# Layer 1 of a two-layer scan-convolution network: result units of one image group with all blocks of h, in place of units of two groups with half of the blocks

## The chip, the cores and the metric

The kernel runs on one core of one Trainium2 chip. The metric is the device time of one execution in microseconds. Three runs of the kernel before took 4558.59 to 4567.19 us, with a median of 4567.16. The profiled execution, from which all other times here come, spans 4551.0 us at a mean granted TensorE clock of 0.964.

## The reference

The input `x` has 32 images, 48 channels, 64 rows (h) and 128 columns (w), in float32. Two layers with weights of their own do the same thing:

```
x = x + SCNN(groupnorm16(x))

SCNN:  down   scan over h, from row 0 to 63
       up     scan over h, from row 63 to 0
       right  scan over w, from column 0 to 127
       left   scan over w, from column 127 to 0

one step of every scan:  nxt = inp + conv1d(carry, w, b)
```

In the down and up scans the convolution runs along w, in the right and left scans along h. It has 48 channels in and out, five taps and zero padding of two. Each step needs the step before it, so a layer is a chain of 63 + 63 + 127 + 127 steps for every image. The last operation of a layer adds its input `x`, the residual, to what the left scan leaves. After layer 1 that sum is the output.

## The kernel before

**Tiles.** The 32 images form four groups of eight (`GB`). One group fills the 512 columns of a matmul together with the eight blocks that a row or a column is cut into. The 384 partitions needed, 8 positions e inside a block times 48 channels, are three sets of 128 (o = 0, 1, 2). Since 48 doesn't divide 128, `pieces(o)` lists the 3 or 4 runs of partitions with one e each: 48, 48 and 32 channels, or 16, 48, 48 and 16.

**Steps.** A step is nine fp32 products on TensorE (L661) and three additions of bias and input on VectorE (L670). The products of the next step read what these additions wrote.

**Phases.** `PHASES` lists twelve, one after the other on TensorE. A "rows" phase does the down and up scans of one group (steps named d and u), a "cols" phase the right and left scans of a pair of groups (r and l). The last three are phase 9 (rows of group 3 in layer 1), phase 10 (columns of groups 0 and 1) and phase 11 (columns of groups 2 and 3). In the profile `step_13u` is the end of phase 9, `step_10r` and `step_10l` are phase 10, and `step_11r` and `step_11l` are phase 11.

**The arena.** One large SBUF tile holds three slots of 6 MB and four staging tiles of 1 MB (`stage`). A slot holds a quarter of w (32 columns) of a pair of groups, that is six units of 128 partitions by 2048 values (`UNITS` numbers them by o and by the half, which is the group in the pair). A column phase has four quarters and three slots: quarter 3 takes the slot of quarter 0. So quarter 0 is written to DRAM after the right scan has passed it (`spill_unit`, `spill<-arena`) and brought back during the left scan (`arena<-spill`). Two column phases in a row use the slots in opposite order, so that the quarters of phase 11 move into slots as phase 10 finishes with them. Their data come from DRAM, where the rows phases left them (`arena<-upb`; the stores are `upb<-arena`).

**Results of layer 1.** The left scan finishes quarters 3, 2, 1 and 0 in this order. Every unit of a quarter then goes through three functions:

- `load_residual` brings the unit's part of the layer's input from DRAM (`mid`) into a "nat" tile. There are three of these: two staging tiles, and the tile `downs`, which holds the weights of the rows scans until phase 9 is over. In layer 1 these loads are on ScalarE's DMA queue (`arena<-mid`, `downs<-mid`).
- `add_permuted` has GpSimd add the residual and put the values in the order of the output, w innermost, into one of two "perm" tiles: eight instructions of 128 by 256 (L621).
- `store_result` writes the perm tile to `out` (`out<-arena`), in runs of 32 values = 128 bytes, half of the transfers on SyncE's queue and half on ScalarE's. For quarters 2, 1 and 0 of phase 10 (`HELD`) it is `hold_result` instead, which writes long runs to a DRAM tile (`held<-arena`, SyncE). `let_result` copies these from DRAM to `out` during phase 11 (`out<-held`).

In layer 1 a unit is (o, r): both groups of the pair, and half (r) of the eight blocks of h. The final quarter of phase 11 is done after the last step by `last_loads` and `last_results` (L892 to L912), which use VectorE for the addition and ScalarE, GpSimd and VectorE for the copies that permute.

**Order.** All this work is entered in an agenda, `at(t, ...)`, with a due time counted in steps: the first three residual loads of a column phase at `left + 16`, where `left` is the first step of the left scan; the addition of unit i of the n-th finished quarter at `left + 34 + 32 n + 4.5 i`; its store or hold five steps later; the let-go copies of phase 10 from `end + 63` on. The agenda is sorted, the steps of the scans are put between, and `in_order` (L193) ties every instruction to the one before it on its engine. So each engine's own order is fixed. How the engines' instructions stand to each other is left to a scheduler. Two things follow from this:

- An engine's queue issues its transfers in order. A transfer that has to wait holds up all that stand behind it on that queue.
- The program has eight completion counters for the transfers of SyncE's and ScalarE's queues together. They are given out in turn in the scheduler's order. A transfer is issued only when the one before it on the same counter has landed, whichever queue that one is on.

Nearly all transfers go through the helper `dma` (L189), so the profile shows them with its line and tells them apart by the names of the tiles. In the changed program the helper stands at L192.

Of the kernel before, what the change touches and what calls it, by code (L numbers as in the profile page):

```python
# [29 lines left out]
F32 = mybir.dt.float32  # L30
AF = mybir.ActivationFunctionType
ALU = mybir.AluOpType

C = 48
# [7 lines left out]
GB = 8  # L42
E8 = 8
FULL = 128
NG = E8 * C // FULL
NQ = 4
# [45 lines left out]
def kernel(  # L92
# [56 lines left out]
    def kept(name):  # L149
# [14 lines left out]
        for i in range(4)  # L164
    ]

    HELD = (2, 1, 0)
    held = {
        j: dram.tile([C, 2 * CHANNEL // NQ], F32, tag=f"held{j}", name=f"held{j}") for j in HELD
    }  # L170

    def by_row(t, e, h0, h1):
# [10 lines left out]
    def by_col(t, e, j):  # L183


        return t.rearrange("c (i q n) -> i q c n", i=E8, q=NQ)[e, j]

    def dma(dst, src, queue=None):
        (queue or nc.sync).dma_start(dst, src)  # L189
# [21 lines left out]
    def pieces(o):  # L211
        return [(e, c0, c1, p0) for e, c0, c1, g, p0 in PIECES if g == o]
# [335 lines left out]
    def quarter(k, j):  # L548
        return slot[slots(k)[j % 3]].rearrange("p (o s n) -> p s o n", s=2, o=NG)
# [22 lines left out]
        else:  # L572
            dma(there, here)

    HH = NH // 2

    def load_residual(k, j, i, nat):
        _, layer, pair = PHASES[k]  # L580
        if layer == 0:
            o, half = UNITS[i]
            t = source[0][2 * pair + half]
            for e, c0, c1, p0 in pieces(o):
                dma(nat[p0 : p0 + c1 - c0], by_col(t, e, j)[c0:c1])
            return
        o, r = divmod(i, 2)
        view = nat.rearrange("p (s n) -> p s n", s=2)
        part = slice(r * HH * LINE, (r + 1) * HH * LINE)
        for e, c0, c1, p0 in pieces(o):  # L590
            for s in range(2):
                dma(
                    view[p0 : p0 + c1 - c0, s],
                    by_col(source[1][2 * pair + s], e, j)[c0:c1, part],
                    nc.scalar,
                )

    def add_residual(k, j, i, nat):
        o, half = UNITS[i]
# [9 lines left out]
                quarter(k, j)[p0 : p0 + c1 - c0, half, o],  # L609
            )  # L610

    def add_permuted(k, j, i, nat, perm, engines):
        o, r = divmod(i, 2)
        res = quarter(k, j)[:, :, o].rearrange(
            "p s (a e k b) -> p a s b k e", a=NH, e=E8, b=GB
        )[:, r * HH : (r + 1) * HH]
        inp = nat.rearrange("p (s a e k b) -> p a s b k e", s=2, a=HH, e=E8, b=GB)
        dst = perm.rearrange("p (a s b k e) -> p a s b k e", a=HH, s=2, b=GB, e=E8)
        for a in range(HH):
            for s in range(2):  # L620
                engines[(2 * a + s) % len(engines)].tensor_tensor(  # L621
                    dst[:, a, s], res[:, a, s], inp[:, a, s], ALU.add
                )

    def store_result(k, j, i, perm):
        pair = PHASES[k][2]
        o, r = divmod(i, 2)
        both = out[2 * pair * GB : 2 * (pair + 1) * GB]
        dst = both.rearrange("b c (a e) w -> e a c b w", e=E8)[..., j * WQ : (j + 1) * WQ]
        src = perm.rearrange("p (a b n) -> p a b n", a=HH, b=2 * GB)  # L630
        for a in range(HH):
            for e, c0, c1, p0 in pieces(o):
                to = nc.sync if a < HH // 2 else nc.scalar
                dma(dst[e, r * HH + a, c0:c1], src[p0 : p0 + c1 - c0, a], to)

    def hold_result(j, i, perm):
        o, r = divmod(i, 2)
        n = 2 * GB * WQ
        dst = held[j].rearrange("c (a e n) -> e c a n", e=E8, n=n)[:, :, r * HH : (r + 1) * HH]
        for e, c0, c1, p0 in pieces(o):  # L640
            dma(dst[e, c0:c1], perm[p0 : p0 + c1 - c0].rearrange("p (a n) -> p a n", n=n))

    def let_result(j, b, part):

        src = held[j][part].rearrange("c (h b n) -> b (c h) n", b=2 * GB, n=WQ)
        dst = out[b, part].rearrange("c h w -> (c h) w")
        dma(dst[:, j * WQ : (j + 1) * WQ], src[b])


    def step(key, weights, b_at, src, inp, dst, whole, part):  # L650
# [89 lines left out]
    def at(t, fn, *args):  # L740
        agenda.append((t, len(agenda), fn, args))
# [68 lines left out]
    def plan_cols(k, t0, prev):  # L810
# [39 lines left out]
        for u, (t, j, i) in enumerate(units):  # L850
            nat = nats[u % ahead]
            o, half = UNITS[i]
            if u < ahead:
                at(left + 16, load_residual, k, j, i, nat)
            elif not (final and j == 0):
                at(units[u - ahead][0] + (3 if layer == 0 else 4.9), load_residual, k, j, i, nat)
            if layer == 0:
                at(t, add_residual, k, j, i, nat)
                at(t + 4, keep_result, k, j, i)
                unit = quarter(k, j)[:, half, o]  # L860
                if half == 0:
                    for b in range(GB):
                        at(t + 5 + b, stats[0].take, j, o, unit, b)
                else:
                    at(t + 1, stats[1].take, j, o, unit)
            elif not (final and j == 0):
                perm = perms[u % 2]
                at(t, add_permuted, k, j, i, nat, perm, [nc.gpsimd])
                if final or j not in held:
                    at(t + 5, store_result, k, j, i, perm)  # L870
                else:
                    at(t + 5, hold_result, j, i, perm)
        if layer == 0:
            t = units[-1][0] + 14
            g = 2 * pair
            spread(t, scaling(f"r{g}", 1, g, stats[0], r_masks), 1)
            spread(t + 20, scaling(f"r{g + 1}", 1, g + 1, stats[1], r_masks), 1)
        if layer and not final:
            for n in range(len(HELD) * 4 * GB):
                n_done, i = divmod(n, 4 * GB)  # L880
                part = slice(i % 2 * C // 2, (i % 2 + 1) * C // 2)
                at(end + 63 + 0.95 * n, let_result, HELD[n_done], i // 2, part)
        if final:
            at(left + 97, last_loads, k)
            at(end + 4, last_results, k)
# [10 lines left out]
    def last_results(k):  # L896

        for i, nat in enumerate(last_tiles(k)):
            o, r = divmod(i, 2)
            part = slice(r * HH * LINE, (r + 1) * HH * LINE)  # L900
            unit = quarter(k, 0)[:, :, o, part]
            nat = nat.rearrange("p (s n) -> p s n", s=2)
            nc.vector.tensor_tensor(unit, unit, nat, ALU.add)
            src = unit.rearrange("p s (a e k b) -> p a s b k e", a=HH, e=E8, b=GB)
            perm = stage[:, i % 4]
            dst = perm.rearrange("p (a s b k e) -> p a s b k e", a=HH, s=2, b=GB, e=E8)
            for a in range(HH):
                for s in range(2):
                    eng = (nc.scalar, nc.gpsimd, nc.vector)[(2 * a + s) % 8 % 3]
                    copy = eng.copy if eng is nc.scalar else eng.tensor_copy  # L910
                    copy(dst[:, a, s], src[:, a, s])  # L911
            store_result(k, 0, i, perm)  # L912


# [227 lines left out]
```

## Time and profile before

| stretch | from, us | to, us | length, us |
|---|---|---|---|
| right scan, phase 10 | 3294.1 | 3593.5 | 299.4 |
| left scan, phase 10 | 3593.5 | 3849.0 | 255.4 |
| right scan, phase 11 | 3848.8 | 4170.6 | 321.8 |
| left scan, phase 11 | 4170.6 | 4426 | 255.4 |
| from the last step to the end | 4426 | 4551.0 | 125 |

A line of the first part of the page gives an engine's busy time, its share of the span and its number of instructions. The second part cuts the span into 40 slices of 114 us; a digit is the busy share in tenths. A line of a timeline gives the start, the length, the engine, the line, the operation with its output and input, the number of instructions in the stretch, and in brackets the idle time ahead of it with what ended it. A line of waits gives what waited, what it waited for, the total in us, the number of waits and the longest. `SPq` and `ACTq` are the queues on which SyncE and ScalarE issue transfers; `PEld` is TensorE's loading of weights.

GpSimd's additions for phase 11 begin at 4232.6 us. From then until the end of the span it adds 18 units, and the last six are added and copied by `last_results`. From 4422.15 to 4461.4 us ScalarE's queue issues the 48 residual loads of `last_loads`.

Transfers by kind, with the size of one and the median time from issue to landing:

| transfer | queue | count | KB each | us to landing |
|---|---|---|---|---|
| residual loads of layer 1 (arena<-mid) | ScalarE | 136 | 192 | 4.5 |
| stores (out<-arena) | SyncE | 120 | 96 | 3.4 |
| stores (out<-arena) | ScalarE | 120 | 96 | 3.2 |
| holds (held<-arena) | SyncE | 36 | 384 | 5.1 |
| let-go copies (out<-held) | SyncE | 96 | 192 | 4.4 |
| quarters (arena<-upb) | SyncE | 96 | 384 | 10.6 |
| spill (spill<-arena) | SyncE | 24 | 1024 | 13.1 |

The table lists the commonest size of each; a piece of 32 or 16 partitions makes smaller ones.

### The profile page before, as it was taken

The numbers are of one execution on the slowest core, as the hardware profiler recorded it, in microseconds if no ns is written. First come the engines' busy times: TensorE is split into PE (matmuls) and PEld (weight loads), VectorE is DVE, ScalarE is ACT, GpSimd is POOL, SyncE is SP. The second block draws the span as 40 slices with busy tenths as digits, with TensorE's granted clock in tenths as the row PEclk, the third lists the DMA queues.
The fourth block names the chain that finished last, engine by engine and source line by source line (L and its number), as shares of the span: only waits on it lengthen the run. The fifth ranks groups of instructions, "written<-read, shape, count | busy, mean of one in ns | idle before, by whom it ended". The sixth has DMA issues, their size and how long they took to land.

```text
span 4551.0 us, 90606 instructions
## 1 busy us (share of the span) xinstructions
PE 4164.5 (92%) x36632; PEld 4133.9 (91%) x36632; DVE 2182.1 (48%) x6594; ACT 1190.0 (26%) x2358; POOL 906.5 (20%) x943
## 2 busy tenths in 40 slices
PE   4899998999999999979999999999969998879990
PEld 1899998999999999979999999999969998879980
DVE  5354443446654444434456654444434444334441
ACT  1743302426776444000035944230000000000000
POOL 4351001314422020000024200000000055500453
PEclk9899998999999999989999999999989999989995
DMA  9989789858979999488048989393097079898789
GB/s 175 177 164 157 115 152 197 198 95 250 213 158 160 160 156 156 75 162 187 1 125 237 200 129 156 45 147 59 9 168 176 1 173 215 188 240 130 158 154 161
DMA packets 2133091, 680.41 MB, mean 150 GB/s; under 512 B 2009792, under 2 KB 2062784, under 8 KB 2101184
## 3 DMA queue, kind: packets, MB, share of 16 engines
q1 hardware_dynamic: 1984832, 602.23, 68.8%
q10 hardware_dynamic: 147840, 72.39, 7.8%
q8 instruction: 288, 4.72, 0.5%
q14 instruction: 131, 1.07, 0.1%
HBM read 397.57 MB, written 295.98 MB: 152 GB/s over the span
## 4 chain that ended last, share of the span: by engine, by line
PE 83%; DMA 9%; POOL 2%; SPq 2%; ACT 1%; issue 1%; ACTq 1%; DVE 1%; POOLq 0%; DVEq 0%
PE step_00r L661 6%; PE step_01r L661 6%; PE step_00l L661 6%; PE step_01l L661 6%; PE step_10r L661 6%; PE step_11l L661 6%; PE step_11r L661 4%; PE step_10l L661 3%; PE step_02u L661 3%; PE step_11d L661 3%; PE step_11u L661 3%; PE step_10u L661 3%; PE step_13u L661 3%; PE step_13d L661 3%; PE step_12u L661 3%; PE step_12d L661 3%
## 5 line engine op out<-in xcount | busy, mean ns | idle before, releaser
L532 ACT ACTIVATE arena<-arena,offset,scale 128x256 f32<-128x256 f32 (+2 forms) x864 | 601.4, 792 | 428.9 <-DMA arena<-mid 174.5
L489 POOL COPY arena<-arena 112x256 f32<-112x256 f32 x458 | 270.7, 647 | 755.4 <-DMA arena<-in_x 459.8
L911 ACT COPY arena<-arena 128x256 f32<-128x256 f32 x18 | 10.4, 643 | 1483.9 <-DMA out<-arena 1475.5
L621 POOL TENSOR_TENSOR arena<-arena 128x256 f32<-128x256 f32 x224 | 232.7, 1082 | 830.7 <-DVE arena L670 733.0
L601 POOL TENSOR_TENSOR arena<-arena 128x2048 f32<-128x2048 f32 x48 | 217.7, 4560 | 833.4 <-PE step_01l L661 537.5
L661 PE MATMUL step_11r<-arena,wright 128*128 128x128 f32 x2286 | 265.0, 280 | 56.9 <-DVE arena L670 30.6
L661 PEld LDWEIGHTS step_11r<-arena,wright 128*128 128x128 f32 x2286 | 263.5, 197 | 58.3 <-DVE arena L670 43.0
L423 ACT ACTIVATE junk<-arena 128x256 f32<-128x256 f32 x192 | 129.5, 675 | 692.6 <-DMA arena<-xin 552.3
L661 PE MATMUL step_10r<-arena,wright 128*128 128x128 f32 x2286 | 261.1, 278 | 38.5 <-DVE arena L670 27.0
L661 PEld LDWEIGHTS step_10r<-arena,wright 128*128 128x128 f32 x2286 | 260.2, 195 | 39.3 <-DVE arena L670 27.5
L661 PE MATMUL step_00r<-arena,wright 128*128 128x128 f32 x2286 | 257.9, 276 | 26.7 <-DMA arena<-upa 26.7
L661 PEld LDWEIGHTS step_00r<-arena,wright 128*128 128x128 f32 x2286 | 257.6, 193 | 27.0 <-issue 26.9
L661 PE MATMUL step_01r<-arena,wright 128*128 128x128 f32 x2286 | 257.3, 276 | 24.5 <-DMA arena<-upa 24.5
L661 PEld LDWEIGHTS step_01r<-arena,wright 128*128 128x128 f32 x2286 | 257.0, 193 | 24.8 <-issue 24.7
L661 PE MATMUL step_00l<-arena,wleft 128*128 128x128 f32 x2286 | 256.3, 275 | 0.0
L661 PEld LDWEIGHTS step_00l<-arena,wleft 128*128 128x128 f32 x2286 | 255.7, 192 | 0.0
L661 PE MATMUL step_11l<-arena,wleft 128*128 128x128 f32 x2286 | 255.4, 275 | 0.0
L661 PE MATMUL step_01l<-arena,wleft 128*128 128x128 f32 x2286 | 255.4, 275 | 0.0
L661 PE MATMUL step_10l<-arena,wleft 128*128 128x128 f32 x2286 | 255.4, 275 | 0.0
L661 PEld LDWEIGHTS step_11l<-arena,wleft 128*128 128x128 f32 x2286 | 255.4, 192 | 0.0
L661 PEld LDWEIGHTS step_01l<-arena,wleft 128*128 128x128 f32 x2286 | 255.3, 192 | 0.0
L661 PEld LDWEIGHTS step_10l<-arena,wleft 128*128 128x128 f32 x2286 | 255.3, 192 | 0.0
(174 smaller groups left out, 7106.1 us busy)
## 6 DMA issues: line engine op xcount, KB each, us to landing
xin<-arena SPq DMA_DIRECT2D x96, 384.0 KB, 5.5
arena<-xin SPq DMA_DIRECT2D x96, 384.0 KB, 8.4
mid<-arena SPq DMA_DIRECT2D x96, 384.0 KB, 7.8
arena<-mid SPq DMA_DIRECT2D x192, 192.0 KB, 4.3
upb<-arena SPq DMA_DIRECT2D x192, 192.0 KB, 4.0
arena<-upb SPq DMA_DIRECT2D x96, 384.0 KB, 10.6
arena<-xin SPq DMA_DIRECT2D x186, 192.0 KB, 4.4
upa<-arena SPq DMA_DIRECT2D x180, 192.0 KB, 3.9
```

Of the source, the lines that this page charges most:

```text
L423: nc.scalar.activation(junk[:, 0:n], view[:, b], AF.Identity, accum_out=self.sum[:, i, j : j + 1])
L489: copy(dst[:, r, q], src[:, r0 + r, q])
L532: nc.scalar.activation(args[0], args[0], AF.Identity, bias=args[2], scale=args[1])
L601: nc.gpsimd.tensor_tensor(unit, unit, nat, ALU.add)
L621: engines[(2 * a + s) % len(engines)].tensor_tensor(dst[:, a, s], res[:, a, s], inp[:, a, s], ALU.add)
L661: nc.tensor.matmul(part(whole(ps[o]), -s), weights[:, i, FULL * (o - NG * s - i + 1) : FULL * (o - NG * s - i + 2)], part(src(i), s), star ...
L911: copy(dst[:, a, s], src[:, a, s])
```

## The change

A unit of layer 1 becomes (o, half), as in layer 0: one group, all eight blocks of h. It is still 128 partitions by 2048 values, and GpSimd's additions are still eight of 128 by 256 to a unit. The purpose is to have fewer and larger transfers:

- A residual load is 3 or 4 transfers with runs of 8 KB, in place of 6 or 8 with runs of 4 KB. It stays on ScalarE's queue.
- A store is 3 or 4 transfers, all on SyncE's queue, in place of 12 or 16 on two queues. Each needs the whole unit, where a transfer before needed two of the eight additions. The runs in `out` stay at 128 bytes.
- A hold is one transfer of 1 MB on ScalarE's queue, in place of 3 or 4 on SyncE's, since `held` is now laid out by units. A let-go copy takes one e of one group: 48 copies in place of 96, with the same bytes in all.
- In layer 1 ScalarE gets a one-element copy, due at `left + 10`, that reads the last column of quarter 3's first block (column 120), which the left scan writes in its seventh step. Since ScalarE's instructions are in order, its residual loads come after that step.
- `last_results` follows the same units. Its copies go to the three engines in turn, a store of a unit stands behind them.

```diff
--- before.py
+++ after.py
@@ -164,9 +164,12 @@
         for i in range(4)
     ]
 
+
     HELD = (2, 1, 0)
     held = {
-        j: dram.tile([C, 2 * CHANNEL // NQ], F32, tag=f"held{j}", name=f"held{j}") for j in HELD
+        (j, half): dram.tile([NG, FULL, UNIT], F32, tag=f"held{j}{half}", name=f"held{j}{half}")
+        for j in HELD
+        for half in range(2)
     }
 
     def by_row(t, e, h0, h1):
@@ -572,28 +575,12 @@
         else:
             dma(there, here)
 
-
-
-    HH = NH // 2
-
     def load_residual(k, j, i, nat):
         _, layer, pair = PHASES[k]
-        if layer == 0:
-            o, half = UNITS[i]
-            t = source[0][2 * pair + half]
-            for e, c0, c1, p0 in pieces(o):
-                dma(nat[p0 : p0 + c1 - c0], by_col(t, e, j)[c0:c1])
-            return
-        o, r = divmod(i, 2)
-        view = nat.rearrange("p (s n) -> p s n", s=2)
-        part = slice(r * HH * LINE, (r + 1) * HH * LINE)
+        o, half = UNITS[i]
+        t = source[layer][2 * pair + half]
         for e, c0, c1, p0 in pieces(o):
-            for s in range(2):
-                dma(
-                    view[p0 : p0 + c1 - c0, s],
-                    by_col(source[1][2 * pair + s], e, j)[c0:c1, part],
-                    nc.scalar,
-                )
+            dma(nat[p0 : p0 + c1 - c0], by_col(t, e, j)[c0:c1], nc.scalar if layer else None)
 
     def add_residual(k, j, i, nat):
         o, half = UNITS[i]
@@ -609,42 +596,41 @@
                 quarter(k, j)[p0 : p0 + c1 - c0, half, o],
             )
 
-    def add_permuted(k, j, i, nat, perm, engines):
-        o, r = divmod(i, 2)
-        res = quarter(k, j)[:, :, o].rearrange(
-            "p s (a e k b) -> p a s b k e", a=NH, e=E8, b=GB
-        )[:, r * HH : (r + 1) * HH]
-        inp = nat.rearrange("p (s a e k b) -> p a s b k e", s=2, a=HH, e=E8, b=GB)
-        dst = perm.rearrange("p (a s b k e) -> p a s b k e", a=HH, s=2, b=GB, e=E8)
-        for a in range(HH):
-            for s in range(2):
-                engines[(2 * a + s) % len(engines)].tensor_tensor(
-                    dst[:, a, s], res[:, a, s], inp[:, a, s], ALU.add
-                )
+    def by_image(t):
+
+        return t.rearrange("p (a e k b) -> p a b k e", a=NH, e=E8, b=GB)
+
+    def by_w(t):
+        return t.rearrange("p (a b k e) -> p a b k e", a=NH, b=GB, e=E8)
+
+    def add_permuted(k, j, i, nat, perm):
+        o, half = UNITS[i]
+        res = by_image(quarter(k, j)[:, half, o])
+        for a in range(NH):
+            nc.gpsimd.tensor_tensor(by_w(perm)[:, a], res[:, a], by_image(nat)[:, a], ALU.add)
+
+    def in_output(j, g, e):
+
+
+        t = out[g * GB : (g + 1) * GB].rearrange("b c (a e) w -> e (c a) b w", e=E8)
+        return t[e, :, :, j * WQ : (j + 1) * WQ]
 
     def store_result(k, j, i, perm):
         pair = PHASES[k][2]
-        o, r = divmod(i, 2)
-        both = out[2 * pair * GB : 2 * (pair + 1) * GB]
-        dst = both.rearrange("b c (a e) w -> e a c b w", e=E8)[..., j * WQ : (j + 1) * WQ]
-        src = perm.rearrange("p (a b n) -> p a b n", a=HH, b=2 * GB)
-        for a in range(HH):
-            for e, c0, c1, p0 in pieces(o):
-                to = nc.sync if a < HH // 2 else nc.scalar
-                dma(dst[e, r * HH + a, c0:c1], src[p0 : p0 + c1 - c0, a], to)
+        o, half = UNITS[i]
+        for e, c0, c1, p0 in pieces(o):
+            dst = in_output(j, 2 * pair + half, e)[c0 * NH : c1 * NH]
+            src = perm[p0 : p0 + c1 - c0].rearrange("p (a b n) -> p a b n", a=NH, b=GB)
+            dma(dst.rearrange("(c a) b n -> c a b n", a=NH), src)
 
     def hold_result(j, i, perm):
-        o, r = divmod(i, 2)
-        n = 2 * GB * WQ
-        dst = held[j].rearrange("c (a e n) -> e c a n", e=E8, n=n)[:, :, r * HH : (r + 1) * HH]
-        for e, c0, c1, p0 in pieces(o):
-            dma(dst[e, c0:c1], perm[p0 : p0 + c1 - c0].rearrange("p (a n) -> p a n", n=n))
-
-    def let_result(j, b, part):
-
-        src = held[j][part].rearrange("c (h b n) -> b (c h) n", b=2 * GB, n=WQ)
-        dst = out[b, part].rearrange("c h w -> (c h) w")
-        dma(dst[:, j * WQ : (j + 1) * WQ], src[b])
+        o, half = UNITS[i]
+        dma(held[j, half][o], perm, nc.scalar)
+
+    def let_result(j, half, e):
+
+        src = held[j, half].rearrange("o p (a b n) -> (o p a) b n", a=NH, b=GB)
+        dma(in_output(j, half, e), src[e * C * NH : (e + 1) * C * NH])
 
 
     def step(key, weights, b_at, src, inp, dst, whole, part):
@@ -865,8 +851,8 @@
                     at(t + 1, stats[1].take, j, o, unit)
             elif not (final and j == 0):
                 perm = perms[u % 2]
-                at(t, add_permuted, k, j, i, nat, perm, [nc.gpsimd])
-                if final or j not in held:
+                at(t, add_permuted, k, j, i, nat, perm)
+                if final or j not in HELD:
                     at(t + 5, store_result, k, j, i, perm)
                 else:
                     at(t + 5, hold_result, j, i, perm)
@@ -875,11 +861,13 @@
             g = 2 * pair
             spread(t, scaling(f"r{g}", 1, g, stats[0], r_masks), 1)
             spread(t + 20, scaling(f"r{g + 1}", 1, g + 1, stats[1], r_masks), 1)
+        if layer:
+
+            at(left + 10, nc.scalar.copy, junk[:, 0:1], quarter(k, 3)[:, 0, 0, RUN - 1 : RUN])
         if layer and not final:
-            for n in range(len(HELD) * 4 * GB):
-                n_done, i = divmod(n, 4 * GB)
-                part = slice(i % 2 * C // 2, (i % 2 + 1) * C // 2)
-                at(end + 63 + 0.95 * n, let_result, HELD[n_done], i // 2, part)
+            todo = [(j, half, e) for j in HELD for half in range(2) for e in range(E8)]
+            for n, what in enumerate(todo):
+                at(end + 63 + 1.9 * n, let_result, *what)
         if final:
             at(left + 97, last_loads, k)
             at(end + 4, last_results, k)
@@ -896,19 +884,14 @@
     def last_results(k):
 
         for i, nat in enumerate(last_tiles(k)):
-            o, r = divmod(i, 2)
-            part = slice(r * HH * LINE, (r + 1) * HH * LINE)
-            unit = quarter(k, 0)[:, :, o, part]
-            nat = nat.rearrange("p (s n) -> p s n", s=2)
+            o, half = UNITS[i]
+            unit = quarter(k, 0)[:, half, o]
             nc.vector.tensor_tensor(unit, unit, nat, ALU.add)
-            src = unit.rearrange("p s (a e k b) -> p a s b k e", a=HH, e=E8, b=GB)
             perm = stage[:, i % 4]
-            dst = perm.rearrange("p (a s b k e) -> p a s b k e", a=HH, s=2, b=GB, e=E8)
-            for a in range(HH):
-                for s in range(2):
-                    eng = (nc.scalar, nc.gpsimd, nc.vector)[(2 * a + s) % 8 % 3]
-                    copy = eng.copy if eng is nc.scalar else eng.tensor_copy
-                    copy(dst[:, a, s], src[:, a, s])
+            for a in range(NH):
+                eng = (nc.scalar, nc.gpsimd, nc.vector)[a % 3]
+                copy = eng.copy if eng is nc.scalar else eng.tensor_copy
+                copy(by_w(perm)[:, a], by_image(unit)[:, a])
             store_result(k, 0, i, perm)
```

## The prediction

> **What bounds the kernel now.** The shares by engine and the slices come first.
>
> ```profile
> PE 4164.5 (92%) x36632; PEld 4133.9 (91%) x36632; DVE 2182.1 (48%) x6594; ACT 1190.0 (26%) x2358; POOL 906.5 (20%) x943
> PE   4899998999999999979999999999969998879990
> DMA  9989789858979999488048989393097079898789
> ```
>
> TensorE is busy 92% of the span, and the edit leaves its 36632 records alone. What can be won is its idle time: the digits 6, 8, 8, 7 in slices 29 to 37, where layer 1's column phases run, and the last 1.1 slices (125 us), where it is done and results still leave. The first 3040 us run the same instructions in the same order in both programs. Next, TensorE's stretches from 3280 us on.
>
> ```profile
> 3306.68 65.44 PE L661 MATMUL step_10r<-arena,wright 128*128 128x112 f32 x570 [11.48 <-DMA arena<-upb]
> 3381.15 1.65 PE L661 MATMUL step_10r<-arena,wright 128*128 128x128 f32 x6 [9.04 <-DVE arena L670]
> 3400.78 192.92 PE L661 MATMUL step_10r<-arena,wright 128*128 128x112 f32 x1702 [17.98 <-DVE arena L670]
> 3593.53 255.43 PE L661 MATMUL step_10l<-arena,wleft 128*128 128x128 f32 x2286
> 3864.93 66.15 PE L661 MATMUL step_11r<-arena,wright 128*128 128x112 f32 x570 [15.07 <-DMA arena<-upb]
> ...
> 4170.55 255.44 PE L661 MATMUL step_11l<-arena,wleft 128*128 128x128 f32 x2286
> ```
>
> A scan without waits takes 255.4 us (both left scans). Right scan 10 runs 3294.1 to 3593.5 = 299.4 us, 44.0 too long: 38.5 idle, the rest matmuls slowed after the pauses. Right scan 11 runs 3848.8 to 4170.55 = 321.75, 66.3 too long. The tail is 4551 - 4426 = 125. These three, 235 us, are all that the edit can touch. Who held the loads? SyncE's queue waits from 3060 to 3320 us, its timeline there, and GpSimd's waits from 3590 to 4060 and from 4170 on:
>
> ```profile
> SPq L189 <- DMA downs<-mid: 195.4, 4, 193.9
> ```
>
> ```profile
> 3078.51 220.98 SPq L189 DMA_DIRECT2D arena<-upb  x20
> 3299.86 55.19 SPq L189 DMA_DIRECT2D upb<-arena  x50
> ```
>
> ```profile
> POOL arena L621 <- DMA held<-arena: 88.9, 4, 40.8
> ```
>
> ```profile
> POOL arena L621 <- DMA out<-arena: 123.2, 18, 38.3
> ```
>
> SyncE stood 193.9 us behind a residual load (downs<-mid) that is not even on its queue, while DMA moved 1 GB/s (3160 to 3280 us, share 0.00). As soon as phase 9 ended it threw out 50 stores that had piled up, ahead of the next quarters. The built program says why: eight completion counters go in turn to the transfers of both queues, and a transfer waits for the one before it on its counter. The scheduler put ScalarE's residual loads of phase 10 far ahead; the one into `downs` waits for the last matmul of phase 9, which reads weights there, and SyncE's load of arena<-upb is next on that load's counter.
>
> **The Trainium skill.** "DMA: Bandwidth & Descriptors", section "Anatomy of one DMA — SWDGE (gpsimd) path", says that DMA engines never wait on semaphores; the issuing sequencer does, and what is queued behind it stands. The trace agrees: 193.9 us of queue, DMA share 0.00. Section "Issuing engines are not separate DMA queues": transfers of all issuers run on the same 16 engines, and a second issuer saves issue time alone. The trace agrees: stores on SyncE alone moved 159 GB/s (3320 to 3360), on both queues 154 (4470 to 4551). Section "Rules for kernel authors" advises to coalesce, with mostly overhead below 64 KB; here 96-KB stores land in 3.2 to 3.4 us and 384-KB holds in 5.1. Section "Specifications" asks for 512 B or more for line rate; the change keeps the 128-B runs of `out`, so I give its stores no better rate: 150 to 160 against 301 GB/s for loads with 8-KB runs (3440 to 3480).
>
> **The change part by part.**
>
> 1. *ScalarE's copy at left + 10.* It reads the seventh step of the left scan, so ScalarE's residual loads come after it, and the far hoisting ends. In the list of the changed program SyncE's two loads behind the stall wait for counters last held by SyncE's own loads. New wait: queued behind it are the residual loads alone, and GpSimd needs the first at left + 62 us (4232.6 - 4170.55), against about 14 us for seven steps: hidden by 45 us. The copy itself is one element: nothing. Gain: stores of phase 9 and loads of quarters 0 to 2 move into the 120 us in which DMA idled. Layer 0's right scans show one pause each, 26.7 and 24.5 us at the start, since their second group has only just been stored; phase 10's groups have long been stored, so even that is absent. I take all 44 (bounds 38, the idle alone, and 44).
>
> 2. *Holds: 3 or 4 of 256 to 384 KB on SyncE become one of 1 MB on ScalarE.* GpSimd adds a unit in 8 x 1.04 = 8.3 us into one of two perm buffers. Its 24 units took 335 us (3655 to 3990), 14.0 each, because holds lay in SyncE's order between loads of phase 11 that wait for quarters these very adds free. Now only residual loads share their queue. A 1-MB hold lands in 13.1 us (price of the 1-MB spill); bounds 5.1 and 22 (its queue full). Pace (8.3 + 13.1)/2 = 10.7 us; three residual buffers, (8.3 + 10.6)/3 = 6.3, don't bind. With S = start of the left scan: quarter 2 is summed at S + 62 + 12 x 10.7 = S + 190, its successor loaded (6 MB at 301 GB/s, 21 us) by S + 215, needed at S + 255. Quarter 1: S + 255, loaded S + 280, needed S + 319. Quarter 0: S + 319; then spill (6 MB) and load (6 MB), which the order puts behind step 31 of right scan 11, 42 us at full rate and some 60 beside holds: S + 361 to 379, needed S + 383. Close: I leave 8 of the 66 standing and take 58 (bounds 31 and 66).
>
> 3. *let_result: 48 of 384 KB for 96 of 192.* The same bytes in 128-B runs: 18.9 MB in 130 us (4060.5 to 4191). They start when quarter 3 is loaded, run into the left scan as now, and end before the first stores at left + 62. Nothing.
>
> 4. *Stores and residual loads of phase 11, and last_results.* A store was 12 to 16 transfers over both queues and could start on half a unit; now 3 or 4 on SyncE, for the whole unit. Lost is the overlap of add and store inside a unit; won, that GpSimd waits for fewer counters and that 48 last loads (39.2 us of ScalarE's queue at 4422) stand ahead of no store: GpSimd idled 38.3 us for that. But DMA is nearly full here: 4240 to 4340 at 0.91, to 4420 at 0.82, 4430 to 4468 and 4470 to 4551 at 1.03 make, with 4420 to 4430 counted full, 91 + 66 + 10 + 39 + 83 = 289 us of work in 311. Packed without holes that saves 22; 8-KB instead of 4-KB runs in 24 MB of loads some 8 more, my estimate. I take 30. Bounds: 0 (whole-unit stores leave as many holes), and 60, if stores at 160 and loads at 301 GB/s cost no more than 6.5 and 3.5 us a unit: 24 x 10.0 + 21 for the spill brought back = 261 from left + 62, so left + 323, against left + 380 now.
>
> 5. *Issue counts* (ScalarE some 340 transfers fewer, SyncE 208) and the DVE add and copies of last_results, same bytes: off the path, beside stores.
>
> Sum: 44 + 58 + 30 = 132; 4567 - 132 = **4435 us**.
>
> **Rivals.**
> - *B, only the stall of phase 9 goes:* DMA is full in 10 left and 11 right, holds land in 20 us, the pace stays near 14, and quarters 1 and 2 are still late. For: share 0.8 to 1.0 in the tail; 60 us of spill and load in a 64-us gap. Against: the longest waits before were for order. 44 + 20 + 10 = 74: 4493.
> - *C, slower:* whole-unit stores wait their turn in one queue with the spill coming back, each 22 us: (8.3 + 22)/2 = 15.2 a unit over 24 units = 364 against 318 now, +46; the same in phase 10 makes 11 right 20 worse; less 44: 4589. For: half-unit starts and the second queue are gone. Against: one queue alone kept 159 GB/s.
> - *D, everything fits:* 44 + 66 + 60 = 170: 4397. Against: 289 us of DMA work in the tail.
>
> **How the numbers follow.** Forecast 0.62, B 0.20, D 0.12, C 0.06. The range runs from D to B, 4393 to 4497, and leaves out C and the edges of the others. Faster by over 0.2%: A, B, D less a little for an order I misread, 0.92; within 0.2%: 0.02; slower: 0.06.
>
> **What would show it.** Step 1: no SyncE wait of over 20 us before 3300, right scan 10 at 255 to 261 us. Step 2: GpSimd's waits for held under 40 us in all, units 10 to 11.5 us apart, right scan 11 at 255 to 275, any pause at quarter 2. Step 4: GpSimd's 18 units of phase 11 at 11 to 12.5 us, tail 85 to 105. I would be wrong if ScalarE's queue, where holds now wait for GpSimd ahead of residual loads, starved GpSimd of residuals, or if a counter shared across queues stalled SyncE anew at the spill.

## The result, and the profile after

The changed kernel takes 4463.35 us (median of four, 4459.08 to 4464.08) against 4564.4 for the kernel before in the same comparison (4558.59 to 4567.19): a ratio of 0.9778, 95% interval 0.9761 to 0.9795, or 101 us less. The forecast was 4435, with a range of 4393 to 4497.

First TensorE's timeline of the changed kernel, to be read beside the six lines of the kernel before. The step function's matmuls have moved to L647.

```profile
3300.03 256.07 PE L647 MATMUL step_10r<-arena,wright 128*128 128x128 f32 x2286
3555.95 255.44 PE L647 MATMUL step_10l<-arena,wleft 128*128 128x128 f32 x2286
3811.22 65.38 PE L647 MATMUL step_11r<-arena,wright 128*128 128x128 f32 x584
3880.09 66.25 PE L647 MATMUL step_11r<-arena,wright 128*128 128x112 f32 x576 [3.50 <-DVE arena L656]
3953.92 128.58 PE L647 MATMUL step_11r<-arena,wright 128*128 128x112 f32 x1126 [7.58 <-DVE arena L656]
4082.34 255.43 PE L647 MATMUL step_11l<-arena,wleft 128*128 128x128 f32 x2286
```

Right scan 10 is now one piece without a pause. Right scan 11 has two short ones, 3.50 us where quarter 1 begins (step 32) and 7.58 where quarter 2 begins (step 64). The stretches, of these two profiled executions:

| stretch | before, us | after, us | gain, us |
|---|---|---|---|
| right scan 10 | 299.5 | 255.9 | 43.6 |
| left scan 10 | 255.3 | 255.3 | 0 |
| right scan 11 | 321.8 | 271.1 | 50.7 |
| left scan 11 | 255.4 | 255.4 | 0 |
| last step to the end | 125.0 | 124.1 | 0.9 |

That is 95 us. The changed kernel's profiled execution came to phase 10 at 3300.0 us, the other at 3294.1, though both run the same instructions until shortly before; over all fourteen profiles of this study that moment lies between 3289 and 3300. So up to some 10 us of a single execution are decided ahead of phase 10, and the stretches tell more than the sum.

SyncE's queue from 3060 to 3320 us, where the kernel before had 193.9 us for one residual load:

```profile
SPq L192 <- DVE arena L656: 126.8, 15, 89.3
SPq L192 <- DMA arena<-upb: 27.3, 21, 2.3
```

No residual load is left in it. The 89.3 us is a wait for rows that phase 9 hadn't computed yet. The 20 loads of quarter 0 already stand ahead of it; the other 40 follow from 3261 us on, and right scan 10 has no pause.

GpSimd's waits from 3550 to 4060 us (the holds were 88.9 us before):

```profile
POOL arena L610 <- DMA held<-arena: 41.9, 7, 7.1
POOL arena L610 <- issue: 24.7, 4, 8.4
POOL arena L610 <- DMA out<-arena: 22.3, 4, 9.8
```

These names understate the holds. From the first hold on (3703 us), 15 of GpSimd's pauses, 98 us in all, end 0.1 to 0.4 us after the landing of a hold: the 41.9, the 24.7 under "issue", and four that the view puts down to results of VectorE which had long been there. Before, it was 91 us in five. So the waits for holds didn't get less in sum; they became many and short.

Now the stretch from the first addition of phase 11 to the end, before and after. A line gives start and end, the length, the busy us of TensorE's matmuls, TensorE's weight loads, VectorE, ScalarE and GpSimd (with the number of instructions), the granted clock, the busy share of the DMA engines and their GB/s:

```profile
4232.00:4551.00 319.00, 193.99 (x1738) 193.80 (x1736) 116.40 (x309) 10.44 (x18) 165.71 (x162) 0.81 0.92 169
```

```profile
4144.00:4462.00 318.00, 193.77 (x1736) 193.58 (x1734) 120.28 (x309) 10.78 (x18) 167.54 (x162) 0.81 0.92 169
```

These two lines are the part of the forecast that failed: the same length, the same share, the same rate.

### The profile page after: what moved, and what is told of

It reads as the page before. It is cut to its first block, busy times and chain, and to the rows that moved or that the text cites. A ratio compares the mean times of both kernels' runs of the same rounds, so it can differ in the third digit from the quotient of the medians.

```text
span 4461.9 us, 89843 instructions
## 1 busy us (share of the span) xinstructions
PE 4157.1 (93%) x36632; PEld 4127.5 (93%) x36632; DVE 2187.4 (49%) x6594; ACT 1190.5 (27%) x2360; POOL 908.3 (20%) x943
## 4 chain that ended last, share of the span: by engine, by line
PE 79%; DMA 10%; SPq 3%; POOL 3%; ACT 3%; issue 1%; DVE 1%; ACTq 0%; POOLq 0%; DVEq 0%
PE step_01r L647 6%; PE step_00r L647 6%; PE step_10r L647 6%; PE step_00l L647 6%; PE step_01l L647 6%; PE step_11l L647 4%; PE step_10l L647 3%; SPq L192 3%; PE step_11r L647 3%; PE step_11d L647 3%; PE step_11u L647 3%; PE step_10u L647 3%; PE step_12d L647 3%; PE step_13u L647 3%; PE step_13d L647 3%; PE step_03d L647 3%
## 5 line engine op out<-in xcount | busy, mean ns | idle before, releaser
L647 PE MATMUL step_00r<-arena,wright 128*128 128x128 f32 x2286 | 257.5, 276 | 27.6 <-DMA arena<-upa 27.6
L647 PEld LDWEIGHTS step_00r<-arena,wright 128*128 128x128 f32 x2286 | 257.1, 193 | 27.9 <-issue 27.7
L647 PE MATMUL step_01r<-arena,wright 128*128 128x128 f32 x2286 | 258.7, 277 | 24.4 <-DMA arena<-upa 24.4
L647 PEld LDWEIGHTS step_01r<-arena,wright 128*128 128x128 f32 x2286 | 258.4, 194 | 24.8 <-issue 24.6
L647 PE MATMUL step_11r<-arena,wright 128*128 128x128 f32 x2286 | 260.2, 278 | 11.1 <-DVE arena L656 11.1
L647 PEld LDWEIGHTS step_11r<-arena,wright 128*128 128x128 f32 x2286 | 259.7, 194 | 11.5 <-DVE arena L656 11.5
L647 PE MATMUL step_00l<-arena,wleft 128*128 128x128 f32 x2286 | 256.3, 275 | 0.0
L647 PE MATMUL step_10r<-arena,wright 128*128 128x128 f32 x2286 | 256.1, 275 | 0.0
L647 PEld LDWEIGHTS step_10r<-arena,wright 128*128 128x128 f32 x2286 | 255.7, 192 | 0.3
L647 PEld LDWEIGHTS step_00l<-arena,wleft 128*128 128x128 f32 x2286 | 255.7, 192 | 0.0
L647 PE MATMUL step_10l<-arena,wleft 128*128 128x128 f32 x2286 | 255.4, 275 | 0.0
L647 PE MATMUL step_01l<-arena,wleft 128*128 128x128 f32 x2286 | 255.4, 275 | 0.0
L647 PE MATMUL step_11l<-arena,wleft 128*128 128x128 f32 x2286 | 255.4, 275 | 0.0
L647 PEld LDWEIGHTS step_10l<-arena,wleft 128*128 128x128 f32 x2286 | 255.4, 192 | 0.0
L647 PEld LDWEIGHTS step_01l<-arena,wleft 128*128 128x128 f32 x2286 | 255.3, 192 | 0.0
L647 PEld LDWEIGHTS step_11l<-arena,wleft 128*128 128x128 f32 x2286 | 255.3, 192 | 0.0
```

Source lines behind the costliest of these rows:

```text
L647: nc.tensor.matmul(part(whole(ps[o]), -s), weights[:, i, FULL * (o - NG * s - i + 1) : FULL * (o - NG * s - i + 2)], part(src(i), s), star ...
```

## The experiments

The theory: ScalarE's copy alone ends the stall of phase 9; the holds' place in order, on SyncE's queue between phase 11's loads, made right scan 11 long; the tail is filled with DMA work. The rivals: it is the size of the transfers that counts; and the tail is a matter of two perm buffers or of waits. Every run was compared with the kernel before on its own chip (4555.6 to 4558.9 us there), and the stretches are from its profile:

| kernel | whole, us | ratio to before (95%) | right 10 | right 11 | tail |
|---|---|---|---|---|---|
| before | 4564.4 | 1 | 299.5 | 321.8 | 125.0 |
| after | 4463.4 | 0.9778 (0.9761-0.9795) | 255.9 | 271.1 | 124.1 |
| e1 no copy | 4504.0 | 0.9878 (0.9862-0.9894) | 298.4 | 269.3 | 124.4 |
| e2 before with copy | 4503.8 | 0.9874 (0.9860-0.9889) | 255.9 | 311.8 | 125.0 |
| e3 holds on SyncE | 4509.2 | 0.9893 (0.9877-0.9910) | 255.9 | 321.3 | 122.8 |
| e4 before, copy, holds on ScalarE | 4493.7 | 0.9849 (0.9831-0.9867) | 256.0 | 301.0 | 126.3 |
| e5 three perms | 4429.7 | 0.9726 (0.9711-0.9740) | 256.0 | 258.2 | 111.3 |
| e6 stores on two queues | 4446.4 | 0.9757 (0.9743-0.9772) | 255.9 | 274.7 | 107.9 |
| e7 no residual in 11 | 4384.6 | 0.9625 (0.9609-0.9641) | 255.9 | 265.5 | 52.3 |
| e8 long runs in 11 | 4389.4 | 0.9634 (0.9615-0.9652) | 256.0 | 269.7 | 46.7 |
| e9 last loads later | 4456.0 | 0.9772 (0.9757-0.9787) | 255.9 | 274.1 | 121.2 |
| f2 two queues, later loads | 4447.5 | 0.9756 (0.9741-0.9770) | 255.9 | 276.1 | 105.2 |
| f3 three perms, later loads | 4447.9 | 0.9756 (0.9741-0.9770) | 256.1 | 255.4 | 129.2 |
| f1 all three | 4444.5 | 0.9745 (0.9729-0.9762) | 255.9 | 260.4 | 118.8 |

Left scan 10 is 255.3 us in all but e1 (259.7) and e5 (256.9). A stretch is read from one trace. In the changed kernel and in e7, e8 and e9, whose edits touch only what comes after right scan 11, that scan still differs by 8.6 us; a difference of that order says little. The expected wholes are in the microseconds of the first comparison. The kernel before took 5.5 to 8.8 us less on the later chips, so the ratios are what to compare.

### The copy: taken away, and alone

```diff
-        if layer:
-            at(left + 10, nc.scalar.copy, junk[:, 0:1], quarter(k, 3)[:, 0, 0, RUN - 1 : RUN])
```

> The changed kernel without ScalarE's one-element copy, so that its residual loads may be placed ahead again. If the copy's place in ScalarE's order is what ended the stall of phase 9: SyncE stands over 100 us behind a residual load before 3300 us, right scan 10 takes 290 to 300 us again, the whole 4500 to 4510 us. If the larger transfers and fewer counters ended it: right scan 10 stays at 256, the whole 4458 to 4470.

The stall is back as it was: right scan 10 at 298.4 us, with pauses of 11.16, 8.30 and 17.81. SyncE's waits from 3060 to 3320 us of this kernel:

```profile
SPq L192 <- DMA downs<-mid: 194.2, 3, 191.8
```

The other way round, the same lines added to the kernel before:

> The kernel before with only the one-element copy added. If the copy alone ended the stall: right scan 10 at 256 us, right scan 11 still 310 to 322 and the tail 125, the whole 4564 - 44 = 4515 to 4525. If the transfers' size is what matters: 4560 to 4567.

Right scan 10 falls to 255.9 with every transfer at its old size. So the copy, one element long, is worth 43 us there, and the larger transfers nothing. The whole is 11 us below the expected range. About 6 of them are the chip's, whose kernel before took 4558.9; right scan 11 also fell by 10.0, little more than the scatter. A possible cause, not tested: the copy stands in phase 11 too, and puts its first three residual loads after the start of the left scan. The kernel before moved these 3 MB during right scan 11; at the 301 GB/s of other loads that is 10 us, an estimate.

### The holds: queue and size apart

```diff
-        dma(held[j, half][o], perm, nc.scalar)
+        dma(held[j, half][o], perm)
```

> The changed kernel with its 1-MB holds on SyncE's queue. If it is the queue of the holds (their place in order between phase 11's loads) that made right scan 11 long: it goes from 271 back to 300 to 322 us, the whole 4490 to 4515. If it is their size: right scan 11 stays at 268 to 275, the whole 4458 to 4470.

Right scan 11 is 321.3, all of the 50 us are back. The timelines of SyncE's queue show the order at work, first with the holds on SyncE, then in the changed kernel:

```profile
3715.53 42.53 SPq L192 DMA_DIRECT2D held<-arena  x5
3758.16 28.12 SPq L192 DMA_DIRECT2D arena<-upb  x10
3787.86 0.34 SPq L192 DMA_DIRECT2D held<-arena  x1
3792.17 26.50 SPq L192 DMA_DIRECT2D arena<-upb  x10
3819.21 33.06 SPq L192 DMA_DIRECT2D held<-arena  x5
```

```profile
3698.37 24.81 SPq L192 DMA_DIRECT2D arena<-spill  x6
3726.36 138.81 SPq L192 DMA_DIRECT2D arena<-upb  x40
```

With the holds between them the first ten loads wait from 3715 to 3758 us for the holds of five units ahead of them. Without them every load goes as soon as its own unit is summed, and all 40 follow one another. The additions themselves are hardly slower: the 24th unit is done 395 us after the start of left scan 10 in e3, 387 in the changed kernel, 396 in the kernel before.

Is the queue enough, with the old sizes? The kernel before with the copy and

```diff
-            dma(dst[e, c0:c1], perm[p0 : p0 + c1 - c0].rearrange("p (a n) -> p a n", n=n))
+            dma(dst[e, c0:c1], perm[p0 : p0 + c1 - c0].rearrange("p (a n) -> p a n", n=n), nc.scalar)
```

> The kernel before with the copy and with its holds, still 3 or 4 to a unit, on ScalarE's queue. If order is all: right scan 11 at 265 to 280 us, the tail 125 as in both kernels, the whole 4460 to 4480, as good as the changed kernel with none of its larger transfers. If size counts: no better than the copy alone, 4510 to 4525.

It isn't: right scan 11 goes from e2's 311.8 to 301.0 and no further. Neither reading was right. What took the place are slower sums: the 24th unit is done 414 us after the start of left scan 10, in e2 after 390. GpSimd's waits of e4 from 3550 to 4080 us:

```profile
POOL arena L621 <- DMA arena<-mid: 76.3, 5, 17.9
POOL arena L621 <- DMA held<-arena: 41.4, 5, 12.8
```

The first line names residual loads, but each of its five waits ends 0.2 to 0.4 us after the landing of a hold; one of the residuals named lands only when GpSimd is already at work again. By landings GpSimd waits 119 us for holds in e4, 89 in e2 and 98 in the changed kernel. ScalarE's queue now carries 6 or 8 residual loads and 3 or 4 holds for a unit, and the hold's pieces stand behind the loads.

From e2 the queue alone gives 10.8 us, the new units with holds on SyncE lose 9.5 (both about the size of the scatter), and both together gain 40.7. The times of the 24th unit tell the two effects apart. With holds on SyncE it comes after 390 to 396 us and right scan 11 takes 312 to 322; with holds on ScalarE and nearly the same sums (386 to 392 in the changed kernel, e1, e6, e8, e9 and f2) it takes 270 to 276. So the order alone is worth 40 to 45 us at equal speed, and in e4 the sums, 27 us later than the changed kernel's, gave most of it back. Which of the new unit's two sides keeps the sums fast, fewer transfers or one hold in place of 3 or 4, was not separated.

### The tail: less work

Two kernels that leave part of phase 11 out. The first returns from `load_residual` at once in phase 11, so that the residual of groups 2 and 3 is not what is added.

> The changed kernel without the 24 residual loads of 1 MB in phase 11: it adds what lies in those buffers, so the residual of groups 2 and 3 is left out. If DMA work fills the tail: 24 x 3.5 = 84 us less work, the tail falls by 50 to 80, the whole 4385 to 4415. If the cycle of two perm buffers sets it: by no more than 15, the whole 4448 to 4465.

The second writes phase 11's results into a DRAM tile in long runs, so that the output of groups 2 and 3 is missing:

```diff
+            if pair == 1:
+                dma(spill[0][i][p0 : p0 + c1 - c0], perm[p0 : p0 + c1 - c0])
+                continue
```

> The changed kernel with the stores of phase 11 in runs of 8 KB into a DRAM tile in place of 128-B runs in the output: the output of groups 2 and 3 is left out. The same 24 MB. If the 128-B runs are what fills DMA: a store costs 3.5 in place of 6.5 us, GpSimd's 8.3 us become the limit, the tail falls to 45 to 70, the whole 4385 to 4410. If the tail were only a matter of waits: 4445 or more.

Tails of 52.3 and 46.7 us, 72 and 77 less, at the low end of what was expected, with the two perm buffers and the one queue as they are. The same columns as above, of e7 and e8:

```profile
4135.00:4381.00 246.00, 193.84 (x1736) 193.65 (x1735) 117.10 (x309) 10.45 (x18) 170.47 (x162) 0.90 0.71 129
```

```profile
4143.00:4383.00 240.00, 193.40 (x1732) 193.21 (x1731) 128.60 (x308) 10.44 (x18) 170.06 (x162) 0.91 0.81 224
```

The second moves all the bytes, at 224 GB/s in place of 169. Removing the residuals and lengthening the runs gain nearly alike, so neither is the single cost of the tail. Both also shorten waits, since every store or load lands sooner, so these two runs alone don't say how much was work and how much was waiting. The next experiments take 13 to 20 us off with the same bytes and runs: at least that much was waiting. "DMA: Bandwidth & Descriptors", section "Specifications" of the Trainium skill, asks for 512 B or more for line rate. e8 agrees for 8-KB runs against 128-B runs (224 and 169 GB/s over the stretch); no run here tries lengths between. The edit left the 128-B runs as they were.

### The tail: the holes

Three perm and two residual buffers, in place of two and three:

```diff
-        nats, perms = (tiles, None) if layer == 0 else (tiles[0:2], tiles[2:4])
+        nats, perms = (tiles, None) if layer == 0 else (tiles[0:1], tiles[1:4])
...
-                perm = perms[u % 2]
+                perm = perms[u % 3]
```

> The changed kernel with three perm and two residual buffers in place of two and three. If the tail is the cycle of two perm buffers (8.3 us of adding and the store of a whole unit): units of phase 11 come 11 to 12 us apart in place of 14.6, the tail falls from 124 to 80 to 100, the whole 4420 to 4445. If the transfers themselves fill it (292 us of DMA work in the 318 us from left + 62 to the end): at most the holes go, the whole 4440 to 4463.

The tail falls to 111.3, not to the 80 to 100 of a cycle of two buffers: holes filled, at 180 GB/s in place of 169. The whole lies in the range of the first reading all the same, because right scan 11, which wasn't the aim, gives another 13 us. It falls to 258.2, with one pause:

```profile
3802.20 129.73 PE L647 MATMUL step_11r<-arena,wright 128*128 128x128 f32 x1160
3934.39 126.15 PE L647 MATMUL step_11r<-arena,wright 128*128 128x112 f32 x1126 [2.46 <-DVE arena L656]
```

GpSimd's waits for holds go from 98 us to under 10. It now waits for residuals, which have one buffer less: 75 us in 14 pauses that end when one lands. The 24th unit of phase 10 is summed after 358 us in place of 387. Of the kernels that compute all of the reference, this one has the lowest ratio: 0.9726 against 0.9778 for the changed one (the interval overlaps that of f1).

Every other transfer of a store on ScalarE's queue:

```diff
-        for e, c0, c1, p0 in pieces(o):
+        for n, (e, c0, c1, p0) in enumerate(pieces(o)):
...
-            dma(dst.rearrange("(c a) b n -> c a b n", a=NH), src)
+            to = nc.scalar if n % 2 else nc.sync
+            dma(dst.rearrange("(c a) b n -> c a b n", a=NH), src, to)
```

> The changed kernel with every other transfer of a store on ScalarE's queue. If whole-unit stores lose time by standing behind each other and behind the returning spill on SyncE's queue: the tail falls by 10 to 25, the whole 4438 to 4455. If DMA work fills the tail: 4455 to 4470.

The tail is 107.9, the ratio 0.9757, as in the reading of one queue's order: all stores on one queue cost 16 us of tail. The rate over the stretch is 179 GB/s in place of 169, with the same bytes. What cost the time is not settled. That reading names stores which stand behind another unit's store or behind the returning spill. Its rival is the shared counters. SyncE's waits for residual loads of the other queue in the changed kernel, from 4080 us to the end, where the kernel before had none:

```profile
SPq L192 <- DMA arena<-mid: 35.0, 8, 16.7
SPq L192 <- DMA downs<-mid: 13.4, 5, 5.0
```

The 16.7 us is at the returning spill (4228 to 4245), with stores behind it, and GpSimd's next unit starts only at 4263, after 26.1 us of idling, when a store lands. In e6 the spill waits for no residual load, and GpSimd's pause there is 13.4 us. A third candidate is the time to issue. The skill's section "Issuing engines are not separate DMA queues" gives a second issuing engine nothing but that. Here the second queue made the tail 16 us shorter, and no run shows that issue time was what it saved.

The loads of the last quarter's residuals stand ahead of GpSimd's last residual loads on ScalarE's queue. There are 20 of them in the changed program (the expectations have 21, and 24 where four loads of another unit go with them), and 40 of the 48 counted in the kernel before. They were then set later:

```diff
-            at(left + 97, last_loads, k)
+            at(left + 116, last_loads, k)
```

> The changed kernel with the 21 loads of last_loads due at left + 116 in place of left + 97, behind the last residual loads. If they still hold GpSimd up, as in the kernel before (now on ScalarE's queue alone, 37 us of GpSimd's waits from 4325 to 4378 us): tail 105 to 115, the whole 4443 to 4455. If DMA work alone fills the tail: 4455 to 4470.

> The changed kernel with stores on two queues and last_loads behind the last residual loads. Stores on two queues left GpSimd one wait of 40.6 us behind 24 of the last loads. If that hole costs time: tail 90 to 102 in place of 108, the whole 4428 to 4442. If DMA only does then what it would do later: tail 105 to 110, the whole 4441 to 4451.

> The changed kernel with three perm and two residual buffers and last_loads behind the last residual loads. If the last loads cost time there too (GpSimd waits of 13.4 and 20.4 us): 4410 to 4424. If not: 4425 to 4440.

> All three: three perm buffers, stores on two queues, last_loads later. If their gains are of different holes and add: right scan 11 at 258 us, tail 85 to 98, the whole 4400 to 4420. If DMA work (292 us in 318) is the floor: tail 98 to 108, the whole 4420 to 4430.

Alone (0.9772 against 0.9778) and with two queues (0.9756 against 0.9757) it changes nothing that the whole shows beyond noise, and both lie in the range of the second reading. GpSimd's last sum ends 3.4 and 2.1 us sooner, and the tail in the trace is shorter by 2.9 and 2.7, within the scatter. With three perm buffers it is worse (0.9756 against 0.9726): the tail goes from 111.3 to 129.2. But there the edit does not do what it was meant to. With two residual buffers the last unit's loads are due still later, so the last quarter's 20 go ahead of the three of that unit, in f3 and f1 alike. ScalarE's queue in f3:

```profile
4317.49 45.44 ACTq L192 DMA_DIRECT2D arena<-mid  x23
4363.02 3.42 ACTq L192 DMA_DIRECT2D downs<-mid  x3
```

VectorE's waits from 4300 us on, in f3:

```profile
DVE arena L894 <- DMA out<-arena: 53.2, 6, 21.7
DVE arena L889 <- DMA arena<-mid: 16.3, 1, 16.3
```

The copies of the last results now wait for stores out of the staging tiles, and the DMA share drops to 0.53 between 4380 and 4400 us. GpSimd's last sum ends 18 us later than in e5. What of this makes the tail longer is read from one trace and not tested. f3 (4447.9) lies in neither range, and f1 (4444.5) in none either: GpSimd waits 39.0 us there for the three late loads. So f1 doesn't show whether the gains of e5 and e6 add; that stays open.

## Why the prediction was right, and where it was wrong

**Step 1, the copy: right.** 44 forecast, 43.6 measured, and e1 and e2 show it from both sides. The mark named for it, no wait of SyncE over 20 us, was too broad: a wait for rows of 89.3 us stands there and does no harm.

**Step 2, the holds: the right cause and nearly the right size, by a way that wasn't the forecast's.** 58 forecast, 50.7 measured, and e3 shows the cause: the holds' place among the loads. The pause at quarter 2 was left at 8 us and is 7.58; there is also one of 3.50 at quarter 1, and 4.6 us of slower matmuls after them. But the faster sums from which the 58 was worked out didn't come. GpSimd's units came (3942.9 - 3618.0)/24 = 13.5 us apart, not 10.7. Its waits for holds, named to be under 40 us, were 98. A 1-MB hold lands in 14.2 us rather than 13.1, but above all the working let the next hold go while one was under way, and they mostly go one at a time. ScalarE's queue in the changed kernel, and GpSimd:

```profile
3735.02 0.34 ACTq L192 DMA_DIRECT2D held<-arena  x1
3749.89 0.34 ACTq L192 DMA_DIRECT2D held<-arena  x1
3765.37 0.34 ACTq L192 DMA_DIRECT2D held<-arena  x1
```

```profile
3735.24 8.28 POOL L610 TENSOR_TENSOR arena<-arena 128x256 f32<-128x256 f32 x8 [4.45 <-DMA held<-arena]
3750.03 8.34 POOL L610 TENSOR_TENSOR arena<-arena 128x256 f32<-128x256 f32 x8 [6.50 <-DMA held<-arena]
3765.51 8.28 POOL L610 TENSOR_TENSOR arena<-arena,downs 128x256 f32<-128x256 f32 x8 [7.14 <-DMA held<-arena]
```

A sum ends at 3743.52; its hold is issued at 3749.89, when the hold before it lands and GpSimd starts anew. In the trace both holds have the same completion counter. So it is with 9 of the 18 holds, and 4 more wait for a residual load that has their counter. A hold goes a median 6.0 us after its sum, and (8.3 + 6.0 + 14.2)/2 = 14.3, near the 13.5 measured. This is read from the trace; no run tests it. The coupling by counters that step 1 removes from phase 9 is what step 2 had left out.

Quarter 2 was summed 218 us after the start of left scan 10 and not 190, all four after 387 and not 319. With the measured times, the working would have had quarter 1 loaded 14 us after it was needed and quarter 0 some 46 to 64. It also waited for a whole quarter before its successor's loads, where these go unit by unit (e3 beside the changed kernel). The two errors went against each other, so that 58 came so near to 50.7 is in part luck. That the new unit was needed too, so as not to slow the sums (e4), the step did not say.

**Step 3, the let-go copies: right.** 136.4 us in place of 130.4, over 31 us after the left scan began; no wait follows from it.

**Step 4, the tail: wrong.** 30 forecast, with bounds of 0 and 60; 0.9 measured. "Packed without holes that saves 22" failed. GpSimd's 18 units took 263 us, 14.6 each, where 11 to 12.5 were forecast and 15.2 measured before. So its last sum came 9.6 us sooner, counted from the start of left scan 11 (325.5 us in place of 335.1). But from there to the end it took 54.0 us in place of 45.4, and all but 0.9 was lost again. The 38.3-us wait that the step pointed to is gone as such, but the last loads still stand ahead of residuals, in 27 transfers of which they are 20. ScalarE's queue in the changed kernel:

```profile
4319.07 59.45 ACTq L192 DMA_DIRECT2D arena<-mid  x27
```

e7 and e8 agree with the premise that DMA work sets the tail, though they don't part it from waits. But there were holes to pack: e5, e6 and f2 take 13, 16 and 20 us off this tail with the same bytes. The edit made new ones while it closed old ones. It put the stores, as whole units, on one queue, and e6 gives 16 us back by a second one, which the step had weighed at nothing. The second of the signs named for being wrong came true: SyncE stalled anew at the spill, 16.7 us, for a residual load with which it shares a counter. Whether that or the order of the stores is the 16 us is open. The 8 us for 8-KB runs of the residual loads don't show either.

**Step 5: right, as far as the stretches show it.** Its part in the time lost after GpSimd's last sum can't be told apart.

The sum: 43.6 + 50.7 + 0.9 = 95 against 132. 29 of the missing 37 us are step 4, 7 are step 2. The measured time lies between the forecast and rival B, but not for B's reason: right scan 11 gained 50.7 where B gave it 20. Rival C saw the stores wait in one queue with the spill. The argument against it, 159 GB/s on one queue, was taken from stores of phase 9, which don't say how long a store waits here; yet the whole didn't become slower.

## What to carry to other kernels

When a queue stands behind a transfer that isn't its own, look for what the two share (here a completion counter) and ask where the scheduler put the other transfer; a one-element instruction that gives it a later place was worth 43 us. Where a queue mixes transfers which free buffers with transfers which fill them, each filling one waits for all that stand ahead of it; parting them was worth 50 us here (e3). Count then how many transfers the other queue has to carry, and look whether two that should overlap share a counter: the holds went one at a time, 13.5 us a unit in place of 10.7. Before forecasting a gain in a stretch whose DMA engines are 0.92 busy, ask which bytes, which short runs or which wait the edit removes, and which new wait it brings.

## What the runs showed of the hardware

The busy share of the DMA engines is not a measure of work left to pack. The same results and residuals took 318 us at a share of 0.92 (169 GB/s), 301 at 1.03 (e6, 179 GB/s), 305 at 0.98 (e5, 180 GB/s) and 312 at 1.08 (f1, 176 GB/s). The products of share and length, 293, 310, 299 and 337 us, differ for bytes that agree to 2% (53.7 to 54.9 MB). The forecast read the share as work: 0.92 as 8% of holes, and 1.03 over 119 us as 122 us of it.
